# Handing projections out in single products, the output bias on VectorE, and spread transposes in a fused decoder layer

## The chip, the cores and the metric

The kernel runs on one core of a Trainium2 chip. The metric is the device time of one launch in microseconds (us), as the median of a few runs of the same program. The engines work in parallel, each through its own queue in program order: TensorE (PE) multiplies matrices, VectorE (DVE), ScalarE (ACT) and GpSimd (POOL) work element by element, and SyncE (SP) issues most of the transfers. Engines wait for each other through semaphores.

## What is computed

One decoder layer in float32 over `x` of 4 batches x 1024 tokens x 512 features, with a context `ctx_768` of 4 x 1024 x 384:

```
x = x + attn(layernorm(x))              # 16 heads of 32, gated softmax, rotated, @ Wout
x = x + xattn(layernorm(x), ctx_768)    # 16 heads of 32, softmax(q k^T) v, @ Wo + bo
x = x + ffn(layernorm(x))               # 512 -> 64, 64 small networks of 16 units, 64 -> 512, + bout

s = einsum('btd,dm->btm', x, Win) + bin_
h = relu(s[..., None] * W1 + b1)
g = einsum('btmh,mh->btm', h, W2) + b2
out = einsum('btm,md->btd', g, Wout) + bout
```

In the first attention the softmax weights are multiplied by one gate per query and one per key and then normalized again, so that two sums over the keys are needed for every query.

## The kernel before, in words

**Units and steps.** The list `order` has eight units: units 0 to 3 are the first attention of the four batches, units 4 to 7 the second one. Each unit has two halves of 512 queries, each half four groups `g` of four heads, and each group eight key tiles `kt` of 128 keys. `attention` makes one step of each `(g, kt)`: 32 steps in a half, 512 in all. In this document (5,1,25) is unit 5, half 1, step 25.

**A step.** `scores` (L570 to L591) multiplies keys by queries into two PSUM tiles `s` of 128 x 1024, two banks each, of which there are two in all; ScalarE takes the exponential of each into a tile `e` (L575, six buffers); VectorE adds the `e` up over the key tiles into `es` (L581 for the second key tile, L583 for the later ones) and, in units 0 to 3, also with the key gate into `eg` (L590, L591). Then `finish` of the step before runs `times`: four products of `e` with the values into `av` (L597) and, where `shared` is true (units 0 to 3 and 7), after every second step the sums of two heads' `e` into `sm` by TensorE (L605). In units 4 to 6 VectorE does all the sums. After the last key tile of a group `normalize` copies `av` away, and a step later, between the scores and `times`, `add_up` (L627) sums `es` over the partitions on TensorE. The divisors go through memory and come back (`divide`, `multiply`, L677), a fixed number of steps later.

**What is placed between the steps.** `beside(u, hf)` lists all other work that runs during one half: the next unit's loads, layer norm, transposes (`tr`, L314) and its projections to keys, queries and values; the output projection of the half before (`project`, called o below) with its residual addition and statistics on VectorE (L766, L770, L771); and in units 5 to 7 the feed-forward part of a finished half: normalize (`norm`, L299), write the rows away (L303), read them back in another order (`load_xT`, L308), transpose them on VectorE (`tr`, L314), multiply by `Win` (`inputs`, L837), sixteen hidden units one after another (`hidden`, ScalarE L854 and VectorE L858/L860), the output product (`outputs`, L871, L877), and the bias `bout`, added to the residual rows (`biased`, L822, on GpSimd).

**A product.** `columns` (L87) multiplies one chunk of 128 features by 128 columns in four column strips at once. It is eight matmul records in the profile and is called a product below. A projection tile needs four products, or three where the input is the context (384 features). They accumulate in one bank of a pair (`bank`, two buffers `f`); after the last one the tile is evacuated (`evacuate`, ScalarE once attention has begun).

**Handing out.** Every entry of the list has a load, the number of products that it holds; light entries have 0, a pause has load 1 and no work. `run` walks the steps and, after each step `n`, hands out entries while

```
while parts and (done + parts[0][0] / 2 <= total * (n + 1) / len(main) or n == len(main) - 1):
```

so the load follows a straight line over the half as closely as the size of the entries allows. `weave(light, items)` spreads the first list evenly over the second one's entries. In `proj`, `values` and `project` the entries are parts of two products (the second of a context tile has one).

**Before and after the steps.** A prologue hands out everything that unit 0 needs at once; after the last step a written-out tail finishes unit 7's second half. The attention of unit 7 has no next unit: little but pauses, the o products and the feed-forward of two halves stand beside its steps.

Of the kernel before, what the change touches and what calls it, by code (L numbers as in the profile page):

```python
# [13 lines left out]
ALU = mybir.AluOpType  # L14
# [49 lines left out]
def moderate_path(tc: tile.TileContext, a: dict, out: bass.AP, flag: bass.AP):  # L64
    nc = tc.nc
    x = a["x"]
    with ExitStack() as st:
# [141 lines left out]
        bout_bc = const.tile([P, D], F32, name="bout_bc")  # L209
# [123 lines left out]
        n = len(order)  # L333
# [15 lines left out]
        def pre(u):  # L349

            ph, b = order[u]
# [77 lines left out]
            def proj(what, g, hf):  # L429
                kind = "ctx" if ph == 1 and what == "k" else "in"  # L430
                n = NCK if kind == "ctx" else NC

                def part(cs):
                    def f():
                        if cs[0] == 0:
                            if "w" + what not in me:
                                fetch(what)
                            me["pj"] = bank()
                        for c in cs:
                            columns(  # L440
                                me["pj"], me["w" + what][:, c, ts(g, P)], me[kind, hf](c),
                                start=(c == 0), stop=(c == n - 1),
                            )
                        if cs[-1] == n - 1:
                            copy(me["pj"])
                    return len(cs), f

                def copy(pj):
                    if what == "k":
                        if g == 0 and hf == 0:  # L450
                            me["k"] = p2.tile([P, NC, T], F32, tag="k", name="k")
                        dst = me["k"][:, g, ts(hf, HALF)]
                    else:
                        if g == 0:
                            me["q", hf] = p3.tile([P, NC, HALF], F32, tag="q", name="q")
                        dst = me["q", hf][:, g, :]
                    evacuate(dst, pj, bqk[:, 0 if what == "q" else 1, g : g + 1] if ph else None)

                return [part(list(range(0, 2))), part(list(range(2, n)))]

            def gates(hf):
                def f():
# [35 lines left out]
            def values(kt):  # L498
                kind = "ctx" if ph == 1 else "in"
                n = NCK if ph == 1 else NC  # L500

                hf, t = divmod(kt, 4)

                def part(cs):
                    def f():
                        if cs[0] == 0:
                            if kt == 0:
                                if "wv" not in me:
                                    fetch("v")
                                me["v"] = p2.tile([P, NT, H, DH], F32, tag="v", name="v")  # L510
                            me["pv"] = bank()
                        for c in cs:
                            columns(
                                me["pv"], me[kind, hf, "t"](c, t), me["wv"][:, c, :],
                                start=(c == 0), stop=(c == n - 1),
                            )
                        if cs[-1] == n - 1:
                            pvh = me["pv"].rearrange("p (h d) -> p h d", d=DH)
                            if ph == 0:
                                ex = me["sw"][:, kt, :, 1].unsqueeze(2).to_broadcast([P, H, DH])  # L520
                                nc.vector.tensor_tensor(me["v"][:, kt], pvh, ex, ALU.mult)
                            else:
                                evacuate(me["v"][:, kt], pvh)
                    return len(cs), f

                return [part(list(range(0, 2))), part(list(range(2, n)))]

            def trs(hf):
                return [[(1 if xt0(hf) else 0, tr(hf, t))] for t in range(4)]
# [194 lines left out]
        def post(u, hf):  # L724

            ph, b = order[u]
            last = (u, hf) == (len(order) - 1, 1)
            me = S[u]
            res = {}
# [19 lines left out]
            def project(t):  # L749
                def part(cs, to=None):  # L750
                    def f():
                        assert me["divided", hf] >= cs[-1]
                        if cs[0] == 0:
                            res["po"] = to() if to else bank()
                            res["po", t] = res["po"]
                        if last:
                            res["po"] = res["po", t]
                        for c in cs:
                            columns(
                                res["po"], me["q", hf][:, c, ts(t, P)], me["wo", hf][:, c, :],  # L760
                                start=(c == 0), stop=(c == NC - 1),
                            )
                        if cs[-1] < NC - 1:
                            return
                        r = res[t]
                        nc.vector.tensor_tensor(r, res["po"], r, ALU.add)  # L766
                        s6 = p2.tile([P, 6], F32, tag="bnst1", name="bnst1")
                        if t == 0:
                            res["mv"] = p2.tile([P, 4, 2], F32, tag="fmv", name="fmv")
                        nc.vector.bn_stats(s6, r)  # L770
                        nc.vector.bn_aggr(res["mv"][:, t, :], s6)  # L771
                        if ph == 0:
                            r2 = p2.tile([P, D], F32, tag="r2", name="r2")
                            nc.gpsimd.tensor_tensor(r2, r, bo_bc, ALU.add)  # L774
                            nc.sync.dma_start(x1b_d[b][4 * hf + t], r2)
                    return len(cs), f
                if last:
                    return [part([0, 1, 2], behind if t > 1 else None), part([3])]
                return [part([0, 1]), part([2, 3])]

            def behind():

# [36 lines left out]
                back(rows_d[b][hf], res["xn"])  # L819

            def biased(t):
                return lambda: nc.gpsimd.tensor_tensor(res[t], res[t], bout_bc, ALU.add)  # L822

            def tr(t):
                def f():
# [88 lines left out]
        def weave(light, items):  # L914

            first, second = sum(light, []), sum(items, [])
            out, done = [], 0
            for n, f in enumerate(first):
                upto = (2 * n + 1) * len(second) // (2 * len(first))
                out += second[done:upto] + [f]  # L920
                done = upto
            return [out + second[done:]]
# [14 lines left out]
        def pause(load):  # L937
            return [[(1, None)] * load]

        n = len(order)  # L940
# [5 lines left out]
        ending = []  # L946
# [6 lines left out]
        def some(half, k):  # L953

            h, half["h"] = half["h"][:k], half["h"][k:]
            return h

        def beside(u, hf):

            last = post(u, 0) if hf else post(u - 1, 1) if u else None  # L960
            end = lambda items: weave(held[0]["h"], items) + held.pop()["out"] if held else items
            if u + 1 == n:
                h, out = held[0]["h"], last["wo"] + last["load"]
                k = min(len(h), 6)
                if hf:
                    ending.append(post(u, 1))
                    out += ending[0]["wo"]
                out += weave(h[0:k], pause(12)) + weave(h[k:], last["o"]) + held.pop()["out"]
                out += (ending[0]["load"] if hf else []) + weave(last["ln"], pause(5)) + last["xT"] + pause(8)
                out += last["tr"] + weave(last["b"], pause(2)) + last["s"] + weave(some(last, 8), pause(14))  # L970
                held.append(last)
                return out
            p = pres[u + 1]
            x, ln, xT, tr, k, q, v = (p[i] for i in ("x", "ln", "xT", "tr", "k", "q", "v"))
            next_ = pres[u + 2] if u + 2 < B else None
            if u + 1 < B:
                if hf == 0:
# [3 lines left out]
                    else:  # L981
                        out = one(fold_bv) + x[1] + k[0][0:1] + [rotate(c) for c in range(NC)]
# [14 lines left out]
            if hf == 0:  # L997
                out = ahead(u + 1, "v") + last["wo"] + p["ctx"][1] + end(k[0] + v[0][0:1]) + last["load"] + v[0][1:2]
                out += last["o"] + weave(last["ln"], v[0][2:])
                if "s" in last:  # L1000
                    out += last["xT"] + weave(last["b"], k[1][0:2]) + last["tr"] + k[1][2:3] + last["s"] + xT[0]
                    held.append(last)
                    return out + weave(some(last, 5), k[1][3:] + v[1][0:2]) + tr[0]
                return out + k[1] + xT[0] + v[1][0:2] + tr[0]
            out = ahead(u + 1, "q") + last["wo"] + end(v[1][2:] + q[0][0:2]) + xT[1]
            out += (ahead(u + 2, "k") if u + 2 < n else []) + last["load"] + q[0][2:3] + last["o"] + tr[1]
            out += weave(last["ln"], q[0][3:] + q[1][0:1])
            out += pres[u + 2]["ctx"][0] if u + 2 < n else []
            if "s" in last:
                out += last["xT"] + weave(last["b"], q[1][1:3]) + last["tr"] + [q[1][3][0:1]] + last["s"]  # L1010
                held.append(last)
                return out + weave(some(last, 3), [q[1][3][1:]])
            return out + q[1][1:]

        p = pres[0]
# [693 lines left out]
```

## Time and profile before

| | |
|---|---|
| median of 3 runs | 2247.48 us (2246.14 to 2248.22) |
| the profiled execution | 2244.28 us |
| its span, first to last instruction | 2242.5 us, 52755 instructions |
| mean granted TensorE clock | 0.992 |
| first score matmul, first matmul of the last step | 115.6 us, 2178.9 us |
| ScalarE busy | 1238.0 us (55%) |
| VectorE busy | 1569.7 us (70%) |
| GpSimd busy | 143.5 us (6%) |

A line of a group has the source line, the engine, the operation, output <- inputs, shapes and count; then the busy time in us and the mean ns of one; then how long the engine was idle just before, and who ended that. A line of the timeline has the start in us from the beginning of the span, the length, and how many instructions were merged into it. A matmul is pipelined and its end is modelled, so that matmuls which wait in the queue can appear inside a longer busy stretch: the distance between the starts of two stages says more than the busy time.

### The profile page before, as it was taken

How to read it: one execution, taken by the hardware profiler on the slowest of the kernel's cores; microseconds unless marked ns; L12 is line 12 of the kernel's file. 1: busy time of each engine (PE TensorE's matmuls, PEld its weight loads, DVE VectorE, ACT ScalarE, POOL GpSimd, SP SyncE). 2: the span in 40 equal slices, each digit the busy share in tenths (PEclk: the TensorE clock that was granted, in tenths of full speed). 3: DMA queues.
4: the chain of work that ended last, by engine and by line, in shares of the span. 5: the costliest groups of instructions: out<-in, count | busy, mean ns of one | idle time of the engine just before them, and what ended most of it. 6: DMA issues, size and time to landing. Idle time of an engine off the chain costs nothing.

```text
span 2242.5 us, 52755 instructions
## 1 busy us (share of the span) xinstructions
PE 2185.6 (97%) x22590; PEld 552.0 (25%) x22590; DVE 1569.7 (70%) x2498; ACT 1238.0 (55%) x1488; POOL 143.5 (6%) x145
## 2 busy tenths in 40 slices
PE   6999999999999999999999999999999999999995
PEld 2322222222222222222222222222222222222222
DVE  3468676797766967567686666868777787856576
ACT  0055545555455554555556565565756566577673
POOL 4000011000000000000000000101000010101010
PEclk9999999999999999999999999999999999999997
DMA  4422223122231221211413032221223142203131
GB/s 112 134 80 50 69 89 106 34 79 69 88 104 35 78 69 46 71 52 41 120 32 104 33 86 63 77 82 45 77 80 103 44 105 68 78 21 102 34 87 40
DMA packets 153305, 161.71 MB, mean 72 GB/s; under 512 B 46202, under 2 KB 91898, under 8 KB 151908
## 3 DMA queue, kind: packets, MB, share of 16 engines
q1 hardware_dynamic: 150380, 156.20, 23.9%
q8 instruction: 179, 2.93, 0.6%
q0 software_dynamic: 2144, 0.98, 0.3%
q10 hardware_dynamic: 536, 1.05, 0.1%
q14 instruction: 66, 0.54, 0.1%
HBM read 115.40 MB, written 42.74 MB: 71 GB/s over the span
## 4 chain that ended last, share of the span: by engine, by line
PE 85%; DVE 6%; ACT 3%; issue 2%; DMA 2%; SPq 1%; DVEq 0%; ACTq 0%; POOL 0%
PE f L87 32%; PE s L570 23%; PE av L597 19%; PE sm L605 6%; DVE es L583 3%; PE sm L627 3%; ACT e L575 2%; SPq L92 1%; DVE g L860 1%; PE f L871 1%; PE f L837 1%; ACT hid L854 1%; DMA sum_d<-both 1%; DMA rec_d<-rec 0%; DVE xT L314 0%
## 5 line engine op out<-in xcount | busy, mean ns | idle before, releaser
L575 ACT ACTIVATE e<-s 128x1024 f32<-128x1024 f32 x1024 | 994.2, 1022 | 716.9 <-PE s L570 534.5
L583 DVE TENSOR_TENSOR es<-es,e 128x1024 f32<-128x1024 f32 x534 | 653.6, 1249 | 277.1 <-ACT e L575 276.6
L570 PE MATMUL s<-q,k 32*64 32x512 f32 x8192 | 620.7, 613 | 7.1 <-ACT e L575 5.4
L597 PE MATMUL av<-e,v 128*32 128x512 f32 x4096 | 554.1, 603 | 0.0
L87 PE MATMUL f<-xT,w 128*32 128x512 f32 x2816 | 331.5, 592 | 0.0
L591 DVE SCALAR_TENSOR_TENSOR eg<-e,sw,eg 128x512 f32<-128x512 f32 x448 | 318.5, 746 | 2.3
L570 PEld LDWEIGHTS s<-q,k 32*64 32x64 f32 x8192 | 136.9, 129 | 459.9 <-ACT e L575 256.6
L581 DVE TENSOR_TENSOR es<-e 128x1024 f32<-128x1024 f32 x89 | 109.5, 1253 | 189.3 <-ACT e L575 181.6
L87 PE MATMUL f<-w,q 128*32 128x512 f32 x1984 | 238.2, 592 | 0.4 <-DVE q L716 0.4
L597 PEld LDWEIGHTS av<-e,v 128*32 128x32 f32 x4096 | 88.5, 108 | 403.8 <-issue 401.1
L87 PEld LDWEIGHTS f<-xT,w 128*32 128x32 f32 x2816 | 92.8, 110 | 210.7 <-issue 203.2
L605 PE MATMUL sm<-e,sw 128*2 128x512 f32 x1024 | 133.3, 592 | 0.0
L774 POOL TENSOR_TENSOR r<-res,bo_bc 128x512 f32<-128x512 f32 x32 | 40.9, 1278 | 1085.2 <-DVE res L766 823.1
L87 PE MATMUL f<-w,xT 128*32 128x512 f32 x896 | 104.9, 592 | 0.6 <-DVE q L280 0.6
L87 PEld LDWEIGHTS f<-w,q 128*32 128x32 f32 x1984 | 65.4, 110 | 149.6 <-issue 143.8
L87 PE MATMUL f<-ctxT,w 128*32 128x512 f32 x768 | 92.3, 592 | 0.0
L87 PE MATMUL f<-w,ctxT 128*32 128x512 f32 x768 | 91.9, 592 | 0.0
L854 ACT ACTIVATE hid<-sT,units 128x256 f32<-128x256 f32 x128 | 76.2, 603 | 23.0 <-DVE g L860 20.2
L627 PE MATMUL sm<-es,ones 128*1 128x512 f32 x348 | 69.0, 591 | 3.9 <-DVE es L583 3.6
L822 POOL TENSOR_TENSOR res<-res,bout_bc 128x512 f32<-128x512 f32 x28 | 59.6, 2136 | 76.9 <-DVE r L299 76.9
L860 DVE SCALAR_TENSOR_TENSOR g<-hid,units,g 128x256 f32<-128x256 f32 x120 | 57.6, 480 | 9.2 <-ACT hid L854 3.8
L677 DVE TENSOR_TENSOR q<-both,recb 128x512 f32<-128x512 f32 x63 | 46.3, 735 | 25.0 <-DMA recb<-rec_d 24.8
(254 smaller groups left out, 1064.9 us busy)
## 6 DMA issues: line engine op xcount, KB each, us to landing
recb<-rec_d SPq DMA_DIRECT2D x252, 64.0 KB
xT<-rows_d SPq DMA_DIRECT2D x60, 256.0 KB
rows_d<-r SPq DMA_DIRECT2D x60, 256.0 KB
w<-in_xattn_Wo SPq DMA_DIRECT2D x9, 1024.0 KB
w<-wout_d SPq DMA_DIRECT2D x8, 1024.0 KB
res<-in_x SPq DMA_DIRECT2D x32, 256.0 KB
x1b_d<-r SPq DMA_DIRECT2D x32, 256.0 KB
res<-x1b_d SPq DMA_DIRECT2D x32, 256.0 KB
```

Source lines behind the costliest of these rows:

```text
L87: nc.tensor.matmul(to[r], lhsT=lhsT[:, j, :] if len(lhsT.shape) == 3 else lhsT[:, r], rhs=rhs, **flags)
L570: nc.tensor.matmul(s[m : m + 64, j, :], lhsT=k[r, g, kt * P + m : kt * P + m + 64], rhs=q[r, g, :], start=True, stop=True,)
L575: nc.scalar.activation(e, s, AF.Exp, scale=SCALE)
L581: nc.vector.tensor_tensor(me["es"][i], me["e", 0][i], es[i], ALU.add)
L583: nc.vector.tensor_tensor(me["es"][i], me["es"][i], es[i], ALU.add)
L591: nc.vector.scalar_tensor_tensor(eg, es[0][:, h, :], gate(kt), eg, ALU.mult, ALU.add)
L597: nc.tensor.matmul(av[r, :], lhsT=me["v"][:, kt, HG * g + h, :], rhs=es[h // 2][:, h % 2, :], start=(kt == 0), stop=(kt == NT - 1),)
L605: nc.tensor.matmul(sm[j * DH : j * DH + sums, :], lhsT=me["sw"][:, t, HG * g + 2 + h, :] if ph == 0 else ones, rhs=me["e", t][1][:, h, :], ...
L627: nc.tensor.matmul(sm[j * DH : j * DH + 1, :], lhsT=ones, rhs=e, start=True, stop=True)
L822: return lambda: nc.gpsimd.tensor_tensor(res[t], res[t], bout_bc, ALU.add)
L854: nc.scalar.activation(hid, res["s"], AF.Relu, bias=units[:, 1, h : h + 1], scale=units[:, 0, h : h + 1])
L860: nc.vector.scalar_tensor_tensor(res["g"], res["hid"], units[:, 2, h - 1 : h], res["g"], ALU.mult, ALU.add)
```

## The change

Three things are changed.

1. Projections to keys, queries and values, and the o products of all but the last half, are listed as four (context: three) entries of one product each, in place of two entries.
2. The bias `bout` is added by VectorE in place of GpSimd, 28 times (seven halves of four tiles).
3. The lists that stand beside units 5 to 7 are put in another order. Beside half 1 of units 4 to 6: before, the read-back of the rows, then the four biases woven into the eight products of two tiles, then the four transposes together, half a tile, `inputs`; after, the biases woven into the four products of one tile, the transposes woven into the four products of the next, half a tile, `inputs`. Beside half 0 of units 5 and 6: the transposes are woven into three products, two products more come before `inputs`, and the biases stand behind it, among the first hidden units. Beside unit 7: the biases come first, among eight pauses, then the transposes, woven into three pauses (there were ten pauses, now there are eleven).

```diff
--- before.py
+++ after.py
@@ proj, values @@
-                return [part(list(range(0, 2))), part(list(range(2, n)))]
+                return [part([c]) for c in range(n)]
@@ project @@
                 if last:
                     return [part([0, 1, 2], behind if t > 1 else None), part([3])]
-                return [part([0, 1]), part([2, 3])]
+                return [part([c]) for c in range(4)]
@@ biased @@
-                return lambda: nc.gpsimd.tensor_tensor(res[t], res[t], bout_bc, ALU.add)
+                return lambda: nc.vector.tensor_tensor(res[t], res[t], bout_bc, ALU.add)
@@ beside, u + 1 == n @@
-                out += (ending[0]["load"] if hf else []) + weave(last["ln"], pause(5)) + last["xT"] + pause(8)
-                out += last["tr"] + weave(last["b"], pause(2)) + last["s"] + weave(some(last, 8), pause(14))
+                out += (ending[0]["load"] if hf else []) + weave(last["ln"], pause(5)) + last["xT"]
+                out += weave(last["b"], pause(8))
+                out += weave(last["tr"], pause(3)) + last["s"] + weave(some(last, 8), pause(14))
@@ beside, next unit 5 to 7 (feed-forward where it is due), hf == 0 @@
                 if "s" in last:
-                    out += last["xT"] + weave(last["b"], k[1][0:2]) + last["tr"] + k[1][2:3] + last["s"] + xT[0]
+                    out += last["xT"] + k[1][0:2] + weave(last["tr"], k[1][2:3]) + [k[1][3][0:2]] + last["s"]
                     held.append(last)
-                    return out + weave(some(last, 5), k[1][3:] + v[1][0:2]) + tr[0]
+                    return out + xT[0] + weave(last["b"] + some(last, 5), [k[1][3][2:]] + v[1][0:2]) + tr[0]
@@ beside, the same, hf == 1 @@
             if "s" in last:
-                out += last["xT"] + weave(last["b"], q[1][1:3]) + last["tr"] + [q[1][3][0:1]] + last["s"]
+                out += last["xT"] + weave(last["b"], q[1][1:2]) + weave(last["tr"], q[1][2:3]) + [q[1][3][0:2]] + last["s"]
                 held.append(last)
-                return out + weave(some(last, 3), [q[1][3][1:]])
+                return out + weave(some(last, 3), [q[1][3][2:]])
```

More of the change, by code (lines that the diff above doesn't have):

```diff
@@ L524, in part @@
                     return len(cs), f
-                return [part(list(range(0, 2))), part(list(range(2, n)))]
+                return [part([c]) for c in range(n)]
             def trs(hf):
```

## The prediction

> **What bounds the kernel now.** First the page: TensorE is busy for 97% of the span, and its idle time before the score matmuls (L570) is only 7.1 us. Then the stages: from the first score to the end of unit 6 it is hardly ever idle.
>
> ```profile
> PE 2185.6 (97%) x22590; PEld 552.0 (25%) x22590; DVE 1569.7 (70%) x2498; ACT 1238.0 (55%) x1488; POOL 143.5 (6%) x145
> ...
> L583 DVE TENSOR_TENSOR es<-es,e 128x1024 f32<-128x1024 f32 x534 | 653.6, 1249 | 277.1 <-ACT e L575 276.6
> L570 PE MATMUL s<-q,k 32*64 32x512 f32 x8192 | 620.7, 613 | 7.1 <-ACT e L575 5.4
> ...
> L822 POOL TENSOR_TENSOR res<-res,bout_bc 128x512 f32<-128x512 f32 x28 | 59.6, 2136 | 76.9 <-DVE r L299 76.9
> ```
>
> ```profile
> 115.60:1215.60 1100.00, 1098.87 (x11522) 273.09 (x11522) 792.74 (x1340) 590.15 (x686) 51.72 (x56) 1.00 0.23 70
> 1215.60:1966.00 750.40, 741.84 (x7656) 183.19 (x7652) 557.55 (x728) 470.36 (x574) 53.63 (x29) 1.00 0.27 74
> 1966.00:2179.00 213.00, 211.74 (x2112) 48.88 (x2108) 127.61 (x205) 151.01 (x188) 14.29 (x10) 1.00 0.22 62
> ```
>
> (Columns: length; busy us and instructions of PE, weight loads, VectorE, ScalarE, GpSimd; clock; DMA share; GB/s.) Read so, TensorE leaves about 11 us. But a waiting matmul hides inside a busy stretch, so I read the starts in TensorE's timeline. An empty step of unit 2:
>
> ```profile
> 690.06 1.11 PE L570 MATMUL s<-q,k 32*64 32x512 f32 x16
> 691.10 1.06 PE L597 MATMUL av<-e,v 128*32 128x512 f32 x8
> 692.34 2.00 PE L570 MATMUL s<-q,k 32*64 32x512 f32 x16 [0.17 <-ACT e L575]
> 694.27 1.07 PE L597 MATMUL av<-e,v 128*32 128x512 f32 x8
> ...
> 697.84 1.11 PE L570 MATMUL s<-q,k 32*64 32x512 f32 x16
> ```
>
> Scores take 691.10 - 690.06 = 1.04 us when nothing holds them. In the step after the empty one they take 694.27 - 692.34 = 1.93: the second half of the scores waits for ScalarE to free its PSUM tile. The 0.89 lost counts as busy. A step with one product, in unit 5:
>
> ```profile
> 1501.15 1.11 PE L570 MATMUL s<-q,k 32*64 32x512 f32 x16
> 1502.20 1.07 PE L597 MATMUL av<-e,v 128*32 128x512 f32 x8
> 1503.08 1.04 PE L87 MATMUL f<-w,ctxT 128*32 128x512 f32 x8
> 1504.05 1.33 PE L570 MATMUL s<-q,k 32*64 32x512 f32 x16
> 1505.32 1.07 PE L597 MATMUL av<-e,v 128*32 128x512 f32 x8
> ```
>
> It lasts 2.90, and the next scores take 1.27. I took the lengths of all 512 steps so. Without sums, two products make 3.76 (185 steps), one 2.90, four 5.47: a product costs 0.86, the rest 2.05. Sums (L605) and `add_up` add 0.86 each, `outputs` 0.86, `inputs` 1.71. What a step lasts beyond this sum is a wait: 74.8 us over all steps, 52.4 in units 0 to 6 and 22.4 in unit 7.
>
> **What the waits cost, by filler.** Call filler all TensorE work of a step besides scores and `av`, in units of 0.86. A step without filler costs itself 2.28 - 2.05 = 0.23 here, 0.25 in most others, and 0.89 in the next: 1.14. A step with one costs 1.27 - 1.04, about 0.22. With two it costs nothing. I wrote down the hand-out of the old list from the loads: units 0 to 6 have 18 steps without filler and 49 with one, 18 x 1.14 + 49 x 0.22 = 31.3. By units, priced against measured: unit 0 5.4 / 5.4, unit 1 4.1 / 4.1, unit 2 4.1 / 3.9, unit 3 2.0 / 2.2, (4,0) 2.7 / 2.5; but (4,1) 4.6 / 7.1, (5,0) and (6,0) together 3.5 / 12.1, (5,1) and (6,1) 5.0 / 15.2. So the rule carries where no feed-forward runs, and 21 us have other causes.
>
> **Part 1, single products.** No TensorE work is added. The load follows the line in steps of 0.86 in place of 1.71: in (4,1) the load is 56 over 32 steps, 1.75 a step, so parts of two leave every eighth step empty, and parts of one give it one product. The same count for the new list in units 0 to 6: 4 steps without filler ((0,0) keeps two, (5,1) and (6,1) one each, step 8) and 41 with one: 4 x 1.14 + 41 x 0.22 = 13.6. **Gain 31.3 - 13.6 = 17.7.** Bounds 14 (a fifth lost where an evacuation stands in the way) and 19. Hiding the new one-product steps is ScalarE's slack: two exponentials take 1.94 of 2.90. Unit 7 has pauses only; its 9 and 8 empty steps stay, and so do its 22.4 us: 0, bounds -2 and 2 for the lists moved there.
>
> A rule of the Trainium skill speaks against this part: "TensorE: Matmul & The Clock Gate", section "The mechanism", says that a weight load overlaps running matmuls only when its row group differs, and a product uses all four. At the 0.11 of a weight load in the row of L87, the 39 steps that newly hold a product would pay 4.3. The trace disagrees, since the one-product step is 3.76 less 0.86 to the digit; by the rule the time would be 2224.
>
> **Part 2, the bias.** GpSimd holds VectorE up while it adds:
>
> ```profile
> 1676.87 2.35 DVE L583 TENSOR_TENSOR es<-es,e 128x1024 f32<-128x1024 f32 x2
> ...
> 1681.02 4.50 DVE L583 TENSOR_TENSOR es<-es,e 128x1024 f32<-128x1024 f32 x2
> ```
>
> ```profile
> 1680.72 3.72 POOL L822 TENSOR_TENSOR res<-res,bout_bc 128x512 f32<-128x512 f32 x2 [0.36 <-DVE r L299]
> ```
>
> ```profile
> 1685.58 0.60 PE L627 MATMUL sm<-es,ones 128*1 128x512 f32 x2 [1.10 <-DVE es L583]
> ```
>
> The two additions take 4.50 in place of 2.35, and TensorE stands in `add_up` until they are done: (5,1,25) loses 2.99, (6,1,25) 2.99, (4,1,25) 2.36, and (5,1,17) 1.39 to a late `es` without GpSimd: 9.7. Over all 28 biases VectorE's instructions are 16.9 us longer than their medians. On VectorE a bias costs 0.69 (nearest row: the residual addition L766, same shape, median 0.684): 28 x 0.69 = 19.3. VectorE's total is even (+2.4), but the place differs: GpSimd started each bias right after `norm`, in steps 21 to 23, before the last `es` of the group; now they follow that `es` in VectorE's queue, and step 24 has no `es`. Behind a bias wait the next `es` and the transposes; nobody waits for the bias before `outputs`. `add_up` should lose most of its wait: I keep 2 of 9.7, **gain 7.7**, bounds 9.7 and, if each half's four biases fall on TensorE in (4,1), (5,1), (6,1), -3 x 2.8 = -8.3.
>
> The Trainium skill, "SBUF — State Buffer", section "Who interferes with whom", calls the pair of ports that VectorE and GpSimd share an exclusive lock: the later one is blocked to the end. At the shortest L822 of 1.28 that would free 28 x 1.28 = 35.8 of VectorE's time, more than the 16.9 measured; TensorE waits for 9.7 of it at most, so the time would be 2218.
>
> **Part 3, transposes.** Their number (0.68 each) is the same; spread, no four stand in a row before an `es`. The read-back takes
>
> ```profile
> 1810.14 1.95 SPq L308 DMA_DIRECT2D xn<-rows_d  x4
> ```
>
> ```profile
> 1817.69 2.49 DVE L314 STREAM_TRANSPOSE xn<-xn 128x512 f32<-128x512 f32 x4 [4.08 <-DMA xn<-rows_d]
> ```
>
> 7.55 from issue to transpose. In (5,1) the issue is at 1688.22 and the transpose at 1703.21, 7.4 of cover; now the first transpose comes two steps (7.5) earlier: cover 0. SP's queue holds the same four issues. A VectorE wait of 4.08 cost TensorE 0.2 in (5,0,25), so I take 0.
>
> The hidden units and `outputs` account for the rest, 21.1 - 9.7 = 11.4. Two products in each step beside two hidden units (2 x 0.60) and two exponentials (1.94) even out (5,0) and (6,0), where old steps had one product and three units. Against it, `outputs` in (5,1,7) now comes right after a tile's last product and waits for its evacuation (0.69 and the wait), and (5,0,30) gets three units. **Gain 2**, bounds -4 and 6.
>
> **Sum.** 17.7 + 7.7 + 2 + 0 = 27. The profiled execution, 2244.3, would become 2217; the median is 3.2 above it: **2220**. The prologue (115.6) and the tail (63.5) keep their work. Ends do not all meet: gains of 13 to 35, 2212 to 2234.
>
> **Rivals.** (a) *VectorE blocks on the read-back, slower.* Place: the first transpose of the half-1 lists, now without cover. Six `e` buffers are three steps, 11 us; a longer wait stops TensorE. It decides where the rows land over 11 us late, some 19 after the issue; at 36 after it, each of three halves loses 17: 51 - 27 = +24, 2271. For it: VectorE's queue is strict and `es` stands behind. Against it: only four transposes wait now, 4.1 at most. Chance 0.06.
> (b) *The waits only move, no change.* VectorE is the bound of units 5 and 6 and keeps TensorE's freed time; with the biases costing 8.3, the hidden units 4 and only half of part 1 gained, 17.7 / 2 - 12.3 = -3.5: 2251. For it: VectorE is busy 15.00 of 15.00 us from 1543 to 1558. Against it: 4.40 of 11.00 from 1689 to 1700. Chance 0.05 for 2243 to 2252.
> (c) *All waits of units 0 to 6 go:* 52 gained, 2195. Single steps still cost 0.22 and `outputs` needs its last unit. Chance 0.04 for under 2212.
> (d) *Half the hand-out's gain is lost to evacuations in mid-step:* 2234 to 2243, 0.05.
>
> **Chances.** The forecast holds 0.80; the range is 2212 to 2234. What a measurement here can tell from no change is 0.2%, 4.5 us. Faster: 0.80 + 0.04 + 0.05 = 0.89; same 0.05; slower 0.06.
>
> **What would show it.** Empty steps such as (4,1,4), (4,1,12), (4,1,20) last 2.90 or more with the next scores at 1.04 to 1.27; units 1 and 2 lose under 0.5 each; no L822 on GpSimd, and `es` pairs stay near 2.35; step 25 of half 1 falls from 7.60 to about 4.6; unit 7 is as long as before. I am wrong if score stages of 1.9 remain as many, if `add_up` still waits for `es`, or if transposes wait over 10 us.

## The result and the profile after

| | before | after |
|---|---|---|
| median | 2247.85 us (2246.14 to 2250.86, 4 runs) | 2227.47 us (2226.16 to 2229.39, 4 runs) |
| profiled execution, its span | 2244.28 us, 2242.5 us | 2228.59 us, 2226.8 us |
| first scores, first matmul of the last step | 115.6 us, 2178.9 us | 115.5 us, 2164.6 us |

The ratio is 0.9911, 95% interval 0.9899 to 0.9922: 20.4 us faster, where 27 had been forecast. The two spans differ by less, 15.7 us; the other 4.7 are taken up below.

The page of after, busy time and groups:

```profile
PE 2171.4 (98%) x22590; PEld 549.3 (25%) x22590; DVE 1563.8 (70%) x2526; ACT 1237.1 (56%) x1488; POOL 83.6 (4%) x117
...
L583 DVE TENSOR_TENSOR es<-es,e 128x1024 f32<-128x1024 f32 x534 | 641.8, 1226 | 253.8 <-ACT e L575 252.2
L570 PE MATMUL s<-q,k 32*64 32x512 f32 x8192 | 609.8, 613 | 6.9 <-ACT e L575 5.5
...
L87 PE MATMUL f<-xT,w 128*32 128x512 f32 x2816 | 334.1, 592 | 2.9 <-DVE res L877 2.4
```

TensorE issues the same 22590 matmuls, and 14 us of busy time are gone: waits that had looked like work. GpSimd's 28 biases have left its 145 instructions, and the 534 `es` additions take 641.8 us in place of 653.6. One line is new as a releaser: two products waited 2.4 us together for the residual addition of `outputs` (L877).

As in the prediction, I took the lengths of all steps and subtracted the sum of their TensorE work; the rest is wait. The prediction's terms against that account, in us of gain:

| term | forecast | between the traces |
|---|---|---|
| single products, units 0 to 4 | 14.1 of the 17.7 | 12.4 |
| bias: (4,1,25), (5,1,25), (6,1,25), (5,1,17) | 7.7 | 9.6 |
| rest of units 5 and 6: single products 3.6, lists and hidden units 2 | 5.6 | -2.4 |
| unit 7 | 0 | -1.0 |
| one stall at (0,0,24) | not foreseen | -4.5 |
| prologue and tail | 0 | 1.4 |
| sum | 27.4 | 15.5 (spans: 15.7) |

The step (4,1,4), empty before, and the start of the next, in TensorE's timeline of after:

```profile
1344.17 1.11 PE L570 MATMUL s<-q,k 32*64 32x512 f32 x16
1345.21 1.07 PE L597 MATMUL av<-e,v 128*32 128x512 f32 x8
1346.09 1.90 PE L87 MATMUL f<-xT,w 128*32 128x512 f32 x16
1347.92 1.11 PE L570 MATMUL s<-q,k 32*64 32x512 f32 x16
1348.97 1.06 PE L597 MATMUL av<-e,v 128*32 128x512 f32 x8
```

It holds two products and lasts 1347.92 - 1344.17 = 3.75; the scores behind it take 1.05, not 1.9. Units 1 and 2 lose 0.31 us each in place of 4.1 and 3.9.

The end of a group in (5,1), VectorE's timeline of after and TensorE's:

```profile
1669.99 2.35 DVE L583 TENSOR_TENSOR es<-es,e 128x1024 f32<-128x1024 f32 x2
1672.27 0.54 DVE L299 TENSOR_SCALAR r<-res,fmv,yi 128x512 f32<-128x512 f32 x1
1672.72 0.68 DVE L822 TENSOR_TENSOR res<-res,bout_bc 128x512 f32<-128x512 f32 x1
1674.62 2.36 DVE L581 TENSOR_TENSOR es<-e 128x1024 f32<-128x1024 f32 x2 [1.22 <-ACT e L575]
```

```profile
1672.41 1.11 PE L570 MATMUL s<-q,k 32*64 32x512 f32 x16
1673.45 1.04 PE L627 MATMUL sm<-es,ones 128*1 128x512 f32 x8
1677.00 1.11 PE L570 MATMUL s<-q,k 32*64 32x512 f32 x16
```

The last pair of `es` takes 2.35 (4.50 before), `add_up` (L627) has no wait, and step 25 lasts 1677.00 - 1672.41 = 4.59, the forecast 4.6. Not all of the 3.0 gained in this step is the bias. Before, step 24 was empty, and the scores of step 25 took 1683.45 - 1681.52 = 1.93 (timeline of before):

```profile
1681.52 2.00 PE L570 MATMUL s<-q,k 32*64 32x512 f32 x16
1683.45 1.03 PE L627 MATMUL sm<-es,ones 128*1 128x512 f32 x4
```

That 0.89 is the price of the empty step, which single products remove.

What went worse stands in steps 4 to 11 of (5,1) and (6,1): they lost 2.5 us in each half before and lose 6.4 now. Before, the first `outputs` (L871) stood alone in (5,1,7), and the step lasted 3.10 (TensorE's timeline of before):

```profile
1614.24 1.11 PE L570 MATMUL s<-q,k 32*64 32x512 f32 x16
1615.28 1.06 PE L597 MATMUL av<-e,v 128*32 128x512 f32 x8
1616.28 1.13 PE L871 MATMUL f<-wout,g 64*128 64x512 f32 x4
1617.34 1.14 PE L570 MATMUL s<-q,k 32*64 32x512 f32 x16
```

(5,1,7) to (5,1,9) of after, timeline of TensorE, ScalarE and VectorE:

```profile
1603.98 1.04 PE L87 MATMUL f<-xT,w 128*32 128x512 f32 x8
1604.95 2.00 PE L871 MATMUL f<-wout,g 64*128 64x512 f32 x4
1605.09 0.69 ACT L278 ACTIVATE q<-f,bqk 128x512 f32<-128x512 f32 x1
...
1606.88 1.11 PE L570 MATMUL s<-q,k 32*64 32x512 f32 x16
1607.93 1.06 PE L597 MATMUL av<-e,v 128*32 128x512 f32 x8
1609.17 2.00 PE L570 MATMUL s<-q,k 32*64 32x512 f32 x16 [0.18 <-ACT e L575]
...
1612.93 1.13 PE L871 MATMUL f<-wout,g 64*128 64x512 f32 x4
1614.51 1.28 DVE L877 TENSOR_TENSOR res<-f,res 128x512 f32<-128x512 f32 x2
1615.25 1.06 PE L87 MATMUL f<-xT,w 128*32 128x512 f32 x8 [1.19 <-DVE res L877]
```

`outputs` takes both banks of `f`. Called right behind a tile's last product, its second matmul waits until ScalarE has emptied that tile's bank (L278, to 1605.78): L871 takes 2.00 where 0.86 is work. Step 8 is empty and has its 0.2 and the scores of 2.0 behind it. In step 9 the next product waits 1.19 until VectorE has emptied the second `outputs`. Step 9 alone loses 2.46 us. Against before, step 7 loses 0.9 more and step 9 1.4 more; the other 1.6 of the 3.9 lie in steps 4 to 6, where products stand beside the last hidden units. ScalarE waits there twice 1.49 us for VectorE's additions (L860), but before it waited as long (1.49 and 1.83), so that the cause of this part is open.

The stall at (0,0,24), timeline of after, VectorE, ScalarE and TensorE:

```profile
205.26 0.69 DVE L677 TENSOR_TENSOR q<-both,recb 128x512 f32<-128x512 f32 x1 [7.88 <-DMA recb<-rec_d]
...
208.53 1.94 ACT L575 ACTIVATE e<-s 128x1024 f32<-128x1024 f32 x2 [2.97 <-DVE eg L591]
...
209.61 1.32 PE L570 MATMUL s<-q,k 32*64 32x512 f32 x8 [2.29 <-ACT e L575]
```

Windows of after there (length; busy us and instructions of PE, weight loads, VectorE, ScalarE, GpSimd; granted clock; DMA share; GB/s):

```profile
207.00:209.00 2.00, 0.32 (x4) 0.00 (x0) 2.00 (x5) 0.47 (x1) 0.00 (x0) 1.00 0.00 0
209.00:211.00 2.00, 1.39 (x12) 0.34 (x16) 2.00 (x4) 1.47 (x2) 0.00 (x0) 0.83 0.00 0
211.00:213.00 2.00, 2.00 (x12) 0.36 (x14) 2.00 (x3) 1.16 (x2) 0.00 (x0) 0.50 0.00 0
213.00:215.00 2.00, 2.00 (x19) 0.34 (x12) 0.94 (x2) 1.03 (x2) 0.00 (x0) 0.81 0.00 0
```

The divisors of the group before came back late, VectorE waited 7.88 us for them with the sums behind it, ScalarE for a free buffer, TensorE 2.29 for ScalarE. Then the granted clock fell to 0.50 and the matmuls took up to twice as long: the step lost 5.0. The same read-back held VectorE for 4.70 in the profile of before, without a wait of TensorE. As to the spans: the profiled run of before lies 3.6 under its median and that of after 1.1 above its own, 4.7 together. The stall can account for the 1.1; why that run of before was short is not shown. How large the stall is in the unprofiled runs of after is open, since they have no trace.

### The profile page after: what moved, and what is told of

It is laid out like the page before. It is cut to its first block, busy times and chain, and to the rows that moved or that the text cites. A ratio compares the mean times of both kernels' runs of the same rounds, so it can differ in the third digit from the quotient of the medians.

```text
span 2226.8 us, 52715 instructions
## 1 busy us (share of the span) xinstructions
PE 2171.4 (98%) x22590; PEld 549.3 (25%) x22590; DVE 1563.8 (70%) x2526; ACT 1237.1 (56%) x1488; POOL 83.6 (4%) x117
## 3 DMA queue, kind: packets, MB, share of 16 engines
q10 hardware_dynamic: 536, 1.05, 0.1%
## 4 chain that ended last, share of the span: by engine, by line
PE 89%; DVE 4%; ACT 2%; SPq 2%; issue 2%; DMA 1%; DVEq 0%; ACTq 0%; POOL 0%
PE f L87 34%; PE s L570 24%; PE av L597 20%; PE sm L605 6%; PE sm L627 3%; ACT e L575 1%; DVE es L583 1%; SPq L92 1%; PE f L871 1%; DVE g L860 1%; PE f L837 1%; DMA sum_d<-both 0%; DVE eg L591 0%; ACT hid L854 0%; DMA rec_d<-rec 0%
## 5 line engine op out<-in xcount | busy, mean ns | idle before, releaser
L583 DVE TENSOR_TENSOR es<-es,e 128x1024 f32<-128x1024 f32 x534 | 641.8, 1226 | 253.8 <-ACT e L575 252.2
L570 PE MATMUL s<-q,k 32*64 32x512 f32 x8192 | 609.8, 613 | 6.9 <-ACT e L575 5.5
L860 DVE SCALAR_TENSOR_TENSOR g<-hid,units,g 128x256 f32<-128x256 f32 x120 | 57.6, 480 | 11.9 <-ACT hid L854 5.8
L627 PE MATMUL sm<-es,ones 128*1 128x512 f32 x348 | 65.1, 591 | 0.0
L677 DVE TENSOR_TENSOR q<-both,recb 128x512 f32<-128x512 f32 x63 | 43.5, 691 | 27.5 <-DMA recb<-rec_d 27.3
L766 DVE TENSOR_TENSOR res<-f,res 128x512 f32<-128x512 f32 x62 | 42.5, 685 | 17.4 <-PE f L87 17.2
```

Of the source, the lines that this page charges most:

```text
L570: nc.tensor.matmul(s[m : m + 64, j, :], lhsT=k[r, g, kt * P + m : kt * P + m + 64], rhs=q[r, g, :], start=True, stop=True,)
L583: nc.vector.tensor_tensor(me["es"][i], me["es"][i], es[i], ALU.add)
L627: nc.tensor.matmul(sm[j * DH : j * DH + 1, :], lhsT=ones, rhs=e, start=True, stop=True)
L677: nc.vector.tensor_tensor(me["q", hf][:, g, :], both[:, 0, :], all_, ALU.mult)
L860: nc.vector.scalar_tensor_tensor(res["g"], res["hid"], units[:, 2, h - 1 : h], res["g"], ALU.mult, ALU.add)
```

## The experiments

Each kernel is compared with before, on the same chip in the same session; sessions differ, so kernels of different sessions are compared by their ratios. (u,h) is a half, and losses are waits beyond the TensorE sum in the profiled run.

**e2_bias**: before, with one word changed.

```diff
-                return lambda: nc.gpsimd.tensor_tensor(res[t], res[t], bout_bc, ALU.add)
+                return lambda: nc.vector.tensor_tensor(res[t], res[t], bout_bc, ALU.add)
```

> Only the bias on VectorE; parts of two and the old lists. Theory: GpSimd's collisions make the es sums late, so step 25 of half 1 in units 4 to 6 falls from 7.0 to 7.6 us to about 4.6 to 5.2: 2247.9 - 8 = 2240; empty steps as before. Rival (VectorE's total work is what counts, and it is even): no change, 2248, or slower by the 2.4 us that VectorE gains.

Measured: 2237.88 us, ratio 0.9963 (0.9951 to 0.9976). The biases cost VectorE 18.6 us (28 of them, forecast 19.3). No `add_up` waits for `es` in step 25 of (5,1) and (6,1) any more; these steps last 5.48, above the expected 4.6 to 5.2, since step 24 is still empty and the scores behind it take 1.93; units 5 and 6 lose 22.8 in place of 27.3, units 0 to 4 22.5 in place of 25.2. The bias alone gives 8.3 by the ratio, against the term of 7.7. (5,1,17), which the prediction counted to this term, loses 1.7, no less than before's 1.4: its late `es` is not the bias's doing.

**e3_no_bias**: after, with the bias back on GpSimd (the same line, the other way round).

> The changed kernel with the bias back on GpSimd (28 of them, in the new lists). Theory: GpSimd again runs ahead of its place in the list, beside the es sums of steps 21 to 23, and the add_up of step 25 waits again: 2227.5 + 8 = 2235, with es pairs of 4 us or more in the trace. Rival (the new place of the lists keeps them apart): 2227.5.

Measured: 2240.34, ratio 0.9963 (0.9951 to 0.9975). Without the bias on VectorE the change keeps 0.37% of its 0.89%. Units 5 and 6 lose 28.0 (after 22.4), unit 7 27.0 (after 23.4). Waits of `add_up` are most of the first; the second is (7,0,0) to (7,0,3), 6.0 in place of 2.4, taken up below.

**e1_singles**: before, with parts of one product (in `proj` and `values`, and the same in `project`) and the half tile in the list kept at two products.

```diff
-                return [part(list(range(0, 2))), part(list(range(2, n)))]
+                return [part([c]) for c in range(n)]
...
-                out += last["xT"] + weave(last["b"], q[1][1:3]) + last["tr"] + [q[1][3][0:1]] + last["s"]
+                out += last["xT"] + weave(last["b"], q[1][1:3]) + last["tr"] + [q[1][3][0:2]] + last["s"]
```

> Only the single products (proj, values, project in parts of one); bias on GpSimd and the lists in the old order. Theory (each part removes its own waits: empty steps by the hand-out, late es sums by the bias): units 0 to 4 lose the same 8 to 14 us as in the changed kernel, the es waits of step 25 in half 1 of units 4 to 6 (about 8 us) stay: 2247.9 - 13 = 2235. Rival (the hand-out does it all, the es waits went because the steps became even): the wait at step 25 is gone and the time is that of the changed kernel, 2227.

Measured: 2239.05, ratio 0.9963 (0.9951 to 0.9975), 8.0 us. Units 0 to 4 lose 14.3 in place of 25.2, so the mechanism is there. The 13 of the expectation is not reached. Units 5 and 6 lose 28.6, more than before's 27.3. Two things stand behind that. The biases on GpSimd still hold `es` up, and step 25 of (5,1) and (6,1) still loses 2.0 (3.0 before). And steps 4 to 11 of these halves lose 6.4 as in after, in place of 2.5, although the lists are the old ones. TensorE and VectorE in (5,1,25) and TensorE in (5,1,7) and (5,1,9) of this kernel:

```profile
1669.54 4.51 DVE L583 TENSOR_TENSOR es<-es,e 128x1024 f32<-128x1024 f32 x2
...
1674.10 0.60 PE L627 MATMUL sm<-es,ones 128*1 128x512 f32 x2 [1.05 <-DVE es L583]
```

```profile
1603.31 2.00 PE L871 MATMUL f<-wout,g 64*128 64x512 f32 x4
...
1613.61 1.07 PE L87 MATMUL f<-xT,w 128*32 128x512 f32 x8 [1.19 <-DVE res L877]
```

**e4_pairs**: after, with parts of two products again (the lines of e1_singles the other way round, and in the list of half 0 the half tile as one entry of two products).

> The changed kernel with parts of two products again; bias on VectorE and the new lists stay. Theory: the 18 empty steps of units 0 to 6 come back at 1.14 us each where 4 were left; units 0 to 4 lose 8 to 14 us again, units 5 and 6 win back what outputs beside single products cost (some 4): 2227.5 + 8 = 2236. Rival (the hand-out is worth nothing, the bias and the lists did it): 2227.5.

Measured: 2239.77, ratio 0.9971 (0.9959 to 0.9982). It holds bias and new lists, and is 6.5 under before by the ratio; the bias alone gave 8.3 by its ratio. So the new lists add nothing to the bias that can be told from nothing. Units 0 to 4 lose 22.6, units 5 and 6 24.7 (22.8 in e2), and steps 4 to 11 of (5,1) and (6,1) lose 2.5 as in before. With e1 this settles where the loss at `outputs` comes from: it goes with the single products, whichever lists are used.

Together: by the ratios single products give 8 alone and 13 on top of the rest (0.9971 to 0.9911); the bias 8 alone and 12 on top of the rest (0.9963 to 0.9911). So each seems to pay more beside the other. For single products that is just clear of the intervals, for the bias it is not. Singles and bias with the lists of before were not run.

**e5_filled**: before, with a useless product into a bank of the pair `f` in each of its 35 steps without filler (units 0 to 7).

```diff
+        def extra(u):
+            k = S[u]["k"]
+            columns(bank(), k[:, 0, 0:P], k[:, 0, 0:HALF], start=True, stop=True)
...
+                if n in EMPTY.get(at, ()):
+                    extra(at[0])
```

> The kernel before, with one useless product (eight matmul records, written to a free bank and never read) added to each of its 35 steps without filler: 18 in units 0 to 6, 17 in unit 7. Theory (such a step waits 1.14 us for ScalarE, with one product only 0.22): 0.86 more work and 0.92 less waiting in each, so no change, 2246 to 2250. Rival (TensorE's work is the bound, the waits are elsewhere): 35 x 0.86 = +30, 2278.

Measured: 2252.81, ratio 1.0017 (1.0007 to 1.0027). 35 products are 35 x 0.86 = 30 us of TensorE work, and 3.8 of them show in the time by the ratio; the forecast was none. (4,1) with four more products lasts 123.9 in place of 123.8, and the eleven products in units 1, 2 and 4 add 0.3 us together. So there an empty step does hold about a product's worth of time that nothing else uses; this is the price of 1.14 tested without moving anything. Elsewhere it holds less: between the profiled runs the stretch from the first scores to the last step grows by 9.4 us (the span by 7.7). Unit 7's 17 products make 4.3 of that, the four in units 5 and 6 3.0, and unit 0's three 1.8, of which 1.7 at (0,0,24).

**e6_outputs_apart**: after, with a pause of one product ahead of `outputs` in half 0 and of two behind it in half 1, so that it stands apart from the tiles' products.

```diff
-            end = lambda items: weave(held[0]["h"], items) + held.pop()["out"] if held else items
+            end = lambda items: weave(held[0]["h"], items) + pause(1 - hf) + held.pop()["out"] + pause(2 * hf) if held else items
```

> The changed kernel with a pause of one product before outputs beside half 0, and of two after it beside half 1, so that no product of a projection tile stands in the same step as outputs. Theory (outputs needs both banks, and a product next to it waits until they are evacuated): (5,1,7) and (5,1,9), which last 4.83 and 7.07, lose 1.0 and 1.6 us of waiting, (5,0,7) 0.9, and the same in unit 6; with the hidden units that shift, 8 to 10 us in all: 2218. Rival (the waits there belong to the chain of hidden units and only move): 2226.

Measured: 2225.22, ratio 0.9892 (0.9875 to 0.9909). Units 5 and 6 lose 16.6 in place of 22.4: with `outputs` apart 5.8 of the loss is gone, and step 9 of (5,1) and (6,1) loses nothing, which confirms the collision in the banks. Steps 4 to 6 of (5,1) still lose 2.3 (after 2.6, before 1.0). Unit 7 loses 27.6 in place of 23.4, 3.9 of that in (7,0,0) to (7,0,3), so the time fell less than the waits removed: by its number it is the rival's 2226, and its interval overlaps that of after.

**e7_apart_3**: e6_outputs_apart, and in (0,0) `divide` and `multiply` come three steps after the sums rather than two.

```diff
-                return 2 if u + 1 < len(order) else 3
+                return 2 if 0 < u + hf and u + 1 < len(order) else 3
```

> As e6_outputs_apart, and in unit 0, half 0, divide and multiply come three steps after their transfers in place of two. Theory (the 5.0 us lost in step (0,0,24) come from VectorE waiting 7.9 us for the divisors, as the steps before became shorter): the step lasts 3.8 in every profile, and the time is 4 to 5 us under e6_outputs_apart. Rival (a late transfer in that one execution): same time as e6_outputs_apart.

Measured: 2223.49, ratio 0.9881 (0.9865 to 0.9898). (0,0,24) to (0,0,27) lose 0.3, and the late read-back no longer holds VectorE. The sum expected too much: in the profile of e6_outputs_apart the place lost 1.5, not 5.0, and by their ratios the two kernels can't be told apart. The size of after's stall is that of one execution. A smaller one is in every profile with single products and a distance of two steps: (0,0,24) loses 1.7 in e1, 2.1 in e3, 1.5 in e6, and nothing in before, e2 and e4.

(7,0,0) to (7,0,3) lose 6.4 in this kernel. Timeline of VectorE, ScalarE and TensorE:

```profile
1925.94 0.71 DVE L314 STREAM_TRANSPOSE xn<-xn 128x512 f32<-128x512 f32 x1 [3.63 <-DMA xn<-rows_d]
...
1934.67 6.89 DVE L583 TENSOR_TENSOR es<-es,e 128x1024 f32<-128x1024 f32 x6
...
1941.48 0.41 DVE L858 TENSOR_SCALAR g<-hid,units,fb 128x256 f32<-128x256 f32 x1
1941.98 0.60 ACT L854 ACTIVATE hid<-sT,units 128x256 f32<-128x256 f32 x1 [2.32 <-DVE g L858]
...
1944.12 2.90 PE L570 MATMUL s<-q,k 32*64 32x512 f32 x16 [2.18 <-ACT e L575]
```

```profile
1942.00:1944.00 2.00, 0.00 (x0) 0.00 (x0) 0.97 (x2) 2.00 (x4) 0.00 (x0) 1.00 0.00 0
...
1946.00:1948.00 2.00, 2.00 (x16) 0.30 (x12) 0.00 (x0) 1.78 (x2) 0.00 (x0) 0.50 0.00 0
```

Read downwards: the first transpose of (6,1) waits for the rows, the `es` behind it run late, six stand in a row; the hidden units' first addition (L858) comes behind them; ScalarE's third unit waits for the buffer that this addition frees, with the exponentials behind it; TensorE waits 2.18 for an exponential, and the clock goes to 0.50. Two runs try to cut this chain at different links.

**e8_units_later**: e7_apart_3, without hidden units at the end of (6,1).

```diff
-                return out + weave(some(last, 3), [q[1][3][2:]])
+                return out + weave(some(last, 3 if u + 2 < n else 0), [q[1][3][2:]])
```

> e7_apart_3, and the list of unit 6, half 1 ends without hidden units (three fewer there, three more among the twelve pauses of (7,0)). In the run before, the first transpose of (6,1) waits 3.63 us for the rows, six es additions then stand in a row (6.89 us), the first addition of the hidden units (L858) behind them, and ScalarE's third hidden unit waits 2.32 for it with the exponentials of (7,0,1) behind; steps 0 to 3 of (7,0) lose 6.4 us where the kernel after loses 2.4. Theory: the hidden units are the link, so without them the exponentials run on and these steps lose 2.5 to 3; the three units find ScalarE free in (7,0). Span 2216.5, median 2220. Rival: the pile of es stops TensorE by itself (add_up, L627, in step 1, and the e buffers), so 6 us stay and the time is that of e7_apart_3, 2223.5.

Measured: 2219.13 (2218.18 to 2219.75), ratio 0.9875 (0.986 to 0.9891). (7,0,0) to (7,0,3) lose 1.3. The same place, VectorE and TensorE:

```profile
1936.13 6.89 DVE L583 TENSOR_TENSOR es<-es,e 128x1024 f32<-128x1024 f32 x6
...
1943.53 2.00 PE L570 MATMUL s<-q,k 32*64 32x512 f32 x16
```

The pile of `es` is as long as before, and the scores no longer wait for it. The hidden units were the link; the rival, that the pile stops TensorE by itself, falls. The evidence is this trace: the ratios of e6, e7 and e8 (0.9892, 0.9881, 0.9875) have intervals that overlap. e8 has the lowest median of the kernels run, 27.7 us under before.

**e9_transposes_later**: e7_apart_3, with the four transposes of the half-1 lists two products later.

```diff
-                out += last["xT"] + weave(last["b"], q[1][1:2]) + weave(last["tr"], q[1][2:3]) + [q[1][3][0:2]] + last["s"]
+                out += last["xT"] + weave(last["b"], q[1][1:2]) + [q[1][2][0:2]] + weave(last["tr"], [q[1][2][2:], q[1][3][0:2]]) + last["s"]
```

> e7_apart_3, and in units 4 to 6, half 1 the four transposes of the read-back rows come two products (3.8 us) later. Theory: the wait of the first transpose for the rows (3.63 us in (6,1) of e7_apart_3) goes, the es behind it are no longer late, and steps 0 to 3 of (7,0) lose about 2.4 in place of 6.4; where other transposes wait as long, the steps behind gain as well: span 2216, median 2219.5. Rival: VectorE has no room left in these halves (31.7 of 37 us busy over the last ten steps of (6,1)), the es stand as late and inputs comes later for the hidden units: 2223.5 or a little more.

Measured: 2230.45, ratio 0.993 (0.9917 to 0.9944): the span is 7.3 longer than that of e7_apart_3, where both theories had it shorter or about equal. TensorE and VectorE in (6,1,30):

```profile
1938.80 0.63 PE L837 MATMUL f<-xn,win 128*32 128x256 f32 x4
1939.33 0.69 DVE L677 TENSOR_TENSOR q<-both,recb 128x512 f32<-128x512 f32 x1
1939.94 2.35 DVE L583 TENSOR_TENSOR es<-es,e 128x1024 f32<-128x1024 f32 x2
1942.21 0.70 DVE L314 STREAM_TRANSPOSE xn<-xn 128x512 f32<-128x512 f32 x1
1942.97 3.29 PE L837 MATMUL f<-xn,win 128*32 128x256 f32 x28 [3.54 <-DVE xn L314]
```

The transposes no longer wait for the rows, but the last of them stands behind two `es` and a multiply when `inputs` already asks for it, and TensorE waits directly: 3.54 there, 8.1 over the three halves. What I had left out is the transposes' other side. Between the rows' arrival and `inputs` there is less room than the four transposes and the `es` between them need, so a delay that VectorE had absorbed was put on TensorE.

## Why the prediction held, and where it did not

**The bound and the price of an empty step: right.** e5_filled put 30 us of work into the empty steps for 3.8 by the ratio, nearly for nothing in units 1, 2 and 4, and these units gave what the count gave: units 1 to 3 8.6 of a forecast 8.8, unit 4 4.2 of 4.2. In unit 7 the price was too high: its filled steps won back 0.56 each of the 0.92.

**Part 1, 17.7: right in units 1 to 4, too high elsewhere.** Unit 0 gave nothing where 1.1 was counted, and (0,0,24) took 4.5 in the profiled run, of which some 1.5 to 2 came with every kernel of single products until the distance was made three steps. In units 5 and 6 the gain was spent again, for the reason below.

**The weight load.** By the rule of the Trainium skill, "TensorE: Matmul & The Clock Gate", section "The mechanism", the newly filled steps were to pay 0.11 each. The trace does not agree: a one-product step of after lasts 2.90 as before, and units 1 and 2 lose 0.3 each in all. That 2224 is nearer to the result than 2220 is owed to another cause.

**Part 2, 7.7: right in the mechanism, and in the number partly by luck.** The four steps gained 9.6, but the bias is behind 6.6 of it at most. The 9.7 held 2 x 0.89 for the scores behind the empty steps (5,1,24) and (6,1,24), which part 1 had counted too, and (5,1,17), which fell from 1.39 to 0.12 with the single products (0.3 in e1, 1.7 in e2). What is left is 2.1 + 2.1 + 2.4 = 6.6, and of the 2 us of wait that I kept nothing stayed. The cost of 0.69 a bias held (18.5 us for 28), and no half was slowed by four of them. The exclusive lock (the Trainium skill, "SBUF — State Buffer", section "Who interferes with whom") would have freed 35.8 of VectorE's time. The traces show less: in e2, where only the bias moved, VectorE's busy total fell by 7.0 (1569.7 to 1562.7) and it took on 18.6, so it was relieved of 25.6, and TensorE's waits in units 0 to 6 fell by 7.2. That is no case against the lock itself. In the collision of (5,1,25) before, each of VectorE's two additions lasted 2.29 and GpSimd's second one 2.25, where VectorE's takes 1.22 undisturbed and GpSimd's shortest 1.28: each waited for the rest of the other's, in turn. The 35.8 took it that VectorE always waits for a whole addition.

**Part 3 and the hidden units, "Gain 2, bounds -4 and 6": the step that failed.** The rest of units 5 and 6 lost 2.4 where 5.6 was expected. (1.8 of the expected 3.6 of single products, the scores behind the empty steps, stand in the row of the bias.) The lists gave nothing: e4 loses 1.9 more in these units than e2. The larger loss goes with the single products. The prediction named the place, `outputs` in (5,1,7) behind a tile's last product, and priced it as the evacuation alone (0.69 and the wait). It missed that `outputs` needs both banks: waiting for one tile going in, holding up the next product going out, with an empty step between. Steps 4 to 11 lose 3.9 more in each of two halves, 7.8 together. Steps 7 and 9, the banks, make 4.5 of that; of the 3.2 in steps 4 to 6 most stays in e6, and its cause is open. With `outputs` moved apart units 5 and 6 lost 5.8 less.

**Transposes at 0: right for the waits, wrong for the reserve.** All 28 wait 13.5 us for rows together, none near the 10 that rival (a) needed, and it fell. But "cover 0" was a real warning: in e3, e6 and e7 the first transpose of (6,1) waits 3.2 to 3.6 for its rows (0.38 in after), and (7,0,0) to (7,0,3) lose 3.6 to 4.0 more than in after. That the late `es` get there by way of the hidden units is shown for e7, by e8. Late rows are not the only way in: in e1 the same six `es` stand in a row after a wait of VectorE of 5.53 for the sums read back (`cs`), and the clock falls there too.

**Rival (b)**, VectorE as the next bound, did not come: the whole was never eaten up. In e6 and e7 some 4 of what units 5 and 6 gained came back as a loss at (7,0,0), behind VectorE's `es`, and in e8 that part is gone again.

**The sum.** By the traces the forecast was 12 too high (27.4 to 15.7); by the medians 7 (27 to 20.4). About 8 of the 12 is units 5 and 6, 4.5 the stall, and the rest is small and of both signs.

## What to carry to other kernels

Price a step by what it leaves idle, not by its work: a product put where TensorE would wait costs little (3.8 of 30 us here by the ratio, 7.7 between the profiled spans), so it pays to look at the grain of the work as well as at its amount. Before handing work out in finer grains, follow each accumulator bank: a stage that takes both buffers of a pair can cost twice when it stands directly between two users of that pair. A step that waits in a strict queue has two sides, what it waits for and who waits behind it; moving it away from the one moves it toward the other.

## What the runs showed of the hardware

The granted clock fell around waits of TensorE of little over 2 us. With waits of 2.29 (after), 2.17 (e1 and e3), 2.15 (e6) and 2.18 us (e7) there came a stretch at 0.50 each time, up to 1.8 us behind the wait's end, in e3 0.2 before it. In after a stage of `av` took 1.94 in it, in place of 1.06. The first slices of e7_apart_3 behind its wait, in windows of half a us:

```profile
1944.00:1944.50 0.50, 0.38 (x4) 0.21 (x8) 0.00 (x0) 0.50 (x2) 0.00 (x0) 1.00 0.00 0
1944.50:1945.00 0.50, 0.50 (x8) 0.00 (x0) 0.00 (x0) 0.50 (x2) 0.00 (x0) 0.63 0.00 0
1945.00:1945.50 0.50, 0.50 (x8) 0.30 (x8) 0.00 (x0) 0.50 (x2) 0.00 (x0) 0.50 0.00 0
```

A slice of mean clock c is at half speed for (1 - c) / 0.5 of its length. Added up so, the stretches last 3.41 us in after, 3.42 in e1, 6.82 in e6 and 6.83 in e3 and e7: one or two times 3.4. Waits of 1.02 to 1.71 us, 27 of them between the first scores and the last step in eleven traces, were never followed by a fall. Length alone does not decide: in e9 a wait of 2.81 was not followed by one within 7 us, and in one of 3.54 the clock fell before the wait ended. The Trainium skill, "TensorE: Matmul & The Clock Gate", section "What's actually happening", has the half rate follow an idle window of about 3.4 us that runs freely. The trace agrees on the unit of 3.4 us, and not on the wait: 2.2 us sufficed five times. So a wait of some 2 us can cost more than twice its length: with the 2.29 the step (0,0,24) lost 5.0.
